# A fixed instruction order on five engines for the opening of a two-layer graph kernel

## The chip, the cores and the metric

The kernel runs on one core of one Trainium2 chip. The metric is the device time of one execution in microseconds (us). The engines are TensorE (PE; PEld is its weight load), VectorE (DVE), ScalarE (ACT), GpSimd (POOL) and SyncE (SP, which here only issues transfers). Each works through its own queue in order, and the engines wait for one another with semaphores.

## The reference

Sixty-four graphs of 256 nodes with 256 features pass through two layers; the adjacency is a 0/1 matrix. Layer 0 is a graph attention layer used twice, then a norm, a feed-forward and a second norm:

```
def _gat(h, adj, W, a, out_features):
    Wh = h @ W;  Wh1 = Wh @ a[:F];  Wh2 = Wh @ a[F:]
    e = leaky_relu(Wh1 + swapaxes(Wh2, 1, 2), 0.2)
    att = softmax(where(adj > 0, e, NEG), axis=1)
    return att @ Wh
h = _gat(_gat(x, adj, W1, a1), adj, W2, a2)
h = layernorm(x + h)
h = layernorm(h + relu(h @ w_ff1 + b_ff1) @ w_ff2 + b_ff2)
```

Layer 1 is relational attention with 8 heads (q, k, one set of values for each relation, of which only relations 0 and 1 occur with a 0/1 adjacency), an output projection, a norm, a feed-forward with gelu, and a norm. All of it is in float32.

## The kernel before

**Units and turns.** Two graphs make a unit of four tiles of 128 nodes; there are 32 units. `turn(y, x, z)` does one software-pipelined step: layer 1 of unit y, layer 0's feed-forward of unit x = y + 1, and the two graph attentions of unit z = y + 2. Inside a turn the order of PE, SP, DVE and ACT is written by hand. The 32 turns are not touched by the change.

**The opening.** Before the first turn the kernel has to load and prepare the weights, and bring unit 0 through all of layer 0, and unit 1 through its two attentions up to the sum that its first norm takes. For each unit these stages are:

- transposes of the adjacency (L726) and of x (L674) on PE, with copies by ACT and DVE;
- `project` (L741 on PE, `xpp`; copies L743 on ACT to `xp`);
- `first_scores` (rows of scores, L750 on PE), the softmax: L767 on ACT (broadcast sums), L769 on DVE (leaky relu), L772 on ACT (exp), L776 on DVE (mask and sum), L780 (reciprocal, with a small sum on POOL), L792 on ACT (scaling of `xp`);
- `first_sums` (L801 on PE, `hpp`; copies L803 on ACT to `hp`), then the same softmax on `hp`;
- `second_sums` (L812 on PE, `ygp`; L815 on DVE adds to `y`);
- the norm: L827 and L828 on DVE (moments), L838 and L839 on POOL (power -1/2), L846 on DVE (`offsets`), L856 on ACT (`applied_norm`).

Unit 0 goes on with the transposes of the normed y (L674, `h1T0`), `first_hidden` (fourteen product steps on PE, L900, each two matmuls; L912 copies on ACT, L909 sums on DVE; relu on ACT), `HiddenOut` (seven products, L989; L975 sums and L997 on DVE), a norm, and transposes `h2T0`. A row of the transposed features is set to one (`with_ones`, a memset on POOL, L686), since the biases of the projections are folded into the weights there. Turn 0 then starts with `Projections`: the steps q1, v1, q2, v2, ... (L1056 on PE), with differences `tq` on DVE (L1024). q1 and v1 read the first half of the features, q2 and the differences need the half with the row of ones.

**The weights.** The dense products use a seven-product scheme for two-by-two blocks, so each weight needs four block sums, made on POOL (`seven`, L573 to L576, and `seven_out`, L585 to L588). The norms' scale and shift are folded into the weights that follow: `shifted` (PE matmuls of one column, L596, and a DVE sum, L599), `scaled` (POOL, L603), and `joined` for q, k and v (row products L613 and L617 on PE; L618, L620, L622 on DVE). `folding()` is a generator that does this in five pieces between the stages. L562 and L656 on DVE subtract the values' weights and biases of relation 0 from those of relation 1.

**What sets the order.** The loads, the set-up of the weights and the opening are traced in program order, and a planner then orders each engine's instructions. In the opening only PE and SP are held to the order as written; on DVE, ACT and POOL the planner may pull an instruction forward or push it back by its own estimate of when it is ready. Buffers come from tagged pools: `wh` (two buffers, for `xp` and `hp`), `e` and `ea` (two each), `q` and `v` (one each), six PSUM banks under one tag.

## Time and profile before

| what | us |
|---|---|
| median of 3 runs | 2977.74 (2977.12 to 2978.61) |
| the profiled execution | 2977.29 |
| its span in the trace | 2975.6 |
| PE busy in the span | 2936.1 |
| DVE, ACT, POOL busy | 2624.7, 1822.6, 635.6 |
| first L1056 of turn 0 / of turn 1 (timeline) | 103.58 / 196.46 |
| PE busy in 60 to 70 us | 5.33 of 10 |

The span runs from the first to the last instruction of the trace; the execution's time contains some 1.7 us more. In the fenced lines L741 is a line of the kernel, `xpp<-gwe,xT` is output from inputs, `x16` a number of instructions; an fp32 matmul counts as two. A line of the windows view has, for one stretch of time, the busy time of PE, PEld, DVE, ACT and POOL, the granted TensorE clock (1.00 is full), the share of the DMA engines, and GB/s. A line of the chain has start, length, engine, output and line.

### The profile page before, as it was taken

The numbers are of one execution on the slowest core, as the hardware profiler recorded it, in microseconds if no ns is written. First come the engines' busy times: TensorE is split into PE (matmuls) and PEld (weight loads), VectorE is DVE, ScalarE is ACT, GpSimd is POOL, SyncE is SP. The second block draws the span as 40 slices with busy tenths as digits, with TensorE's granted clock in tenths as the row PEclk, the third lists the DMA queues.
The fourth block names the chain that finished last, engine by engine and source line by source line (L and its number), as shares of the span: only waits on it lengthen the run. The fifth ranks groups of instructions, "written<-read, shape, count | busy, mean of one in ns | idle before, by whom it ended". The sixth has DMA issues, their size and how long they took to land.

```text
span 2975.6 us, 58457 instructions
## 1 busy us (share of the span) xinstructions
PE 2936.1 (99%) x22192; PEld 2501.2 (84%) x22192; DVE 2624.7 (88%) x5024; ACT 1822.6 (61%) x3803; POOL 635.6 (21%) x930
## 2 busy tenths in 40 slices
PE   7999999999999999999999999999999999999997
PEld 6788888888888888888888888888888888888876
DVE  5788999988999989898989999889999898989886
ACT  4466666656656666666666666666566566666653
POOL 4122121221211221211221212212112212112211
PEclk8999999999999999999999999999999999999999
DMA  5011111111111111111111112111112111111000
GB/s 151 14 32 34 36 33 26 42 35 37 35 34 28 42 35 37 32 26 40 39 35 35 33 26 42 35 36 35 36 26 42 35 37 32 27 38 35 19 10 16
DMA packets 416883, 105.36 MB, mean 35 GB/s; under 512 B 360746, under 2 KB 416084, under 8 KB 416596
## 3 DMA queue, kind: packets, MB, share of 16 engines
q1 hardware_dynamic: 415196, 100.23, 15.5%
q8 instruction: 177, 2.90, 0.4%
q0 software_dynamic: 1056, 1.05, 0.1%
q14 instruction: 110, 0.90, 0.1%
q10 hardware_dynamic: 344, 0.28, 0.0%
HBM read 56.78 MB, written 16.78 MB: 25 GB/s over the span
## 4 chain that ended last, share of the span: by engine, by line
PE 96%; DVE 2%; ACT 1%; DMA 1%; issue 0%; POOL 0%; SPq 0%; POOLq 0%; DVEq 0%; ACTq 0%
PE yf L989 26%; PE h1a L900 15%; PE h1b L900 11%; PE po L1104 8%; PE v L1056 7%; PE qk L1056 6%; PE sp L1076 5%; PE yop L812 4%; PE xpp L741 4%; PE hpp L801 4%; PE ygp L812 3%; PE zo L1107 2%; PE rows L750 1%; DMA wf<-in_L_gnn_w_ff_dram 0%; DVE s L776 0%
## 5 line engine op out<-in xcount | busy, mean ns | idle before, releaser
L1089 DVE TENSOR_TENSOR ea<-e,aT 128x1024 f32<-128x1024 f32 x256 | 307.0, 1211 | 4.2 <-ACT e L1085 4.2
L1085 ACT ACTIVATE e<-sp 128x512 f32<-128x512 f32 x512 | 277.2, 606 | 51.7 <-PE sp L1076 35.8
L856 ACT ACTIVATE y<-y,nm,rs 128x256 f32<-128x256 f32 x450 | 243.1, 596 | 98.9 <-DVE nm L846 94.2
L912 ACT COPY h<-h1b 128x512 f32<-128x512 f32 x262 | 152.7, 583 | 192.7 <-PE h1b L900 191.0
L711 POOL COPY hT<-yt 32x256 f32<-32x256 f32 x244 | 237.4, 973 | 139.0 <-DVE yt L694 131.4
L1043 ACT COPY qk<-qk 128x512 f32<-128x512 f32 x128 | 74.3, 581 | 290.4 <-PE qk L1056 289.0
L918 ACT ACTIVATE h<-h,cols 128x256 f32<-128x256 f32 x512 | 220.8, 498 | 31.4 <-DVE h L909 31.4
L909 DVE TENSOR_TENSOR h<-h1a,h 128x512 f32<-128x512 f32 x262 | 176.2, 682 | 53.1 <-PE h1a L900 43.7
L838 POOL TENSOR_SCALAR rs<-mv 128x4 f32<-128x4 f32 (+1 forms) x134 | 33.9, 253 | 872.4 <-DVE mv L828 296.7
L997 DVE TENSOR_TENSOR y<-yf,y 128x256 f32<-128x256 f32 x448 | 185.5, 414 | 34.0 <-PE yf L989 33.7
L827 DVE BATCH_NORM_STATS2 st<-y 128x6 f32<-128x256 f32 x512 | 208.3, 409 | 5.6
L1117 POOL TENSOR_TENSOR low<-low,rq 128x16 f32<-128x16 f32 x64 | 13.9, 217 | 781.8 <-DVE rq L1116 781.8
L743 ACT COPY xp<-xpp 128x260 f32<-128x260 f32 x128 | 44.2, 368 | 212.0 <-PE xpp L741 211.9
L868 DVE TENSOR_TENSOR y<-y,rb 128x1024 f32<-128x1024 f32 (+1 forms) x130 | 166.0, 1277 | 2.2
L865 DVE TENSOR_TENSOR y<-y,rg 128x1024 f32<-128x1024 f32 (+1 forms) x130 | 162.0, 1246 | 1.2 <-ACT y L856 1.1
L1094 DVE TENSOR_TENSOR es<-e 128x1024 f32<-128x1024 f32 x128 | 155.7, 1217 | 0.0
L1076 PE MATMUL sp<-qk 32*128 32x256 f32 x2048 | 146.6, 400 | 0.0
L1104 PE MATMUL po<-e,v 128*32 128x256 f32 x2048 | 136.3, 384 | 2.1 <-DVE qk L1124 2.1
L839 POOL TENSOR_TENSOR rs<-rs,mhalf 128x4 f32<-128x4 f32 (+1 forms) x134 | 134.6, 1004 | 8.4
L1104 PE MATMUL po<-ea,v 128*32 128x256 f32 x2048 | 134.0, 379 | 0.0
L1076 PEld LDWEIGHTS sp<-qk 32*128 32x128 f32 x2048 | 92.5, 184 | 47.6 <-ACT e L1085 12.8
L900 PE MATMUL h1a<-tt,wf 128*128 128x256 f32 x512 | 131.3, 380 | 0.8 <-DVE h L909 0.8
(284 smaller groups left out, 7783.9 us busy)
## 6 DMA issues: line engine op xcount, KB each, us to landing
hT<-yt SPq DMA_DIRECT2D x852, 32.0 KB, 1.9
y<-in_x_dram SPq DMA_DIRECT2D x32, 512.0 KB, 4.6
xq<-in_x_dram SPq DMA_DIRECT2D x240, 64.0 KB, 2.2
aq<-in_adj_dram SPq DMA_DIRECT2D x240, 64.0 KB, 2.4
out_dram<-y SPq DMA_DIRECT2D x30, 512.0 KB, 2.8
wf<-in_L_gnn_w_ff_dram SPq DMA_DIRECT2D x2, 1024.0 KB, 7.4
w<-in_L_gnn_W_dram SPq DMA_DIRECT2D x2, 1024.0 KB, 7.8
first<-in_adj_dram POOLq DMA_DIRECT2D x2, 512.0 KB, 8.1
```

What stands on the lines that cost most here:

```text
L711: nc.gpsimd.tensor_copy(to, at)
L812: nc.tensor.matmul(ps[:, i * F:(i + 1) * F], lhs(t, k), rhs(b, k), start=(k == 0), stop=(k == n - 1))
L827: nc.vector.bn_stats(st[:, t, :], y[:, t, :])
L856: mark["normed"] = nc.scalar.activation(y[:, t, :], y[:, t, :], AF.Identity, bias=nm[:, t:t + 1], scale=rs[:, t:t + 1])
L900: nc.tensor.matmul(ps[:, i * N:(i + 1) * N], w_[:, f * P:(f + 1) * P], m, start=first and i == 0, stop=True, skip_group_check=True)
L918: nc.scalar.activation(y, y if ps is None else ps[:, i * N:(i + 1) * N], func, bias=bi[:, f:f + 1])
L989: nc.tensor.matmul(s.ps[n][:, i * F2:(i + 1) * F2], a[:, k, i * P:(i + 1) * P], w_[:, k, :], start=n in (1, 2, 5) and i == 0 and k == 0, s ...
L1056: nc.tensor.matmul(ps[:, i * N:(i + 1) * N], l, r, start=n in (1, 2, 5) and i == 0, stop=True, skip_group_check=True)
L1076: nc.tensor.matmul(ps[a][:, j * N:(j + 1) * N], k_[hp, m, j0:j0 + P], q[hp, m, b * N:(b + 1) * N], start=True, stop=True)
L1085: nc.scalar.activation(e[:, a, :], ps[a], AF.Exp, scale=isd)
L1089: nc.vector.tensor_tensor(ea[:, a:a + 2, :], e[:, a:a + 2, :], ab[:, None, :].to_broadcast([P, 2, NB * N]), ALU.mult)
L1104: nc.tensor.matmul(po[hp, m * N:(m + 1) * N], vs[:, hp], w[:, a, j * N:(j + 1) * N], start=(n == 0), stop=(n == len(terms) - 1))
```

## The change

The opening is written out as one order for five engines (PE, SP, DVE, ACT, POOL), and the generator `folding()` goes away: its pieces stand as calls between the stages. In the new order

- unit 0's x is transposed inside the set-up of the attention weights, and its adjacency is transposed one graph at a time around `project(0)`;
- unit 0 goes through `project`, softmax, `first_sums`, softmax before `project(1)` starts; unit 1's first softmax stands among the steps of unit 0's norm, its `first_sums` between the hidden steps, its second softmax between the hidden steps and the output products;
- the POOL sums of a weight become an iterator, of which `made(ops, n)` issues the next n; they stand between the steps, and so do `shifted`, `scaled` and `joined`, whose row products on PE are issued apart from the DVE part;
- the subtractions L562 and L656 and the sums of the bias rows (L651) move from the set-up to after the first hidden steps;
- the squares that check the adjacency (L733) go to the front of ACT's order and write to a buffer of tag `ea` instead of in place; unit 1's second scores take the buffer of tag `q`;
- the transposes ahead of both feed-forward and projections are issued in halves (`turned`), followed by the copies (`features`);
- at the end, unit 1's `second_sums` is issued one graph at a time around the halves of `h2T0`, and `with_ones` is written after both POOL steps of unit 1's norm.

The arithmetic is the same; no instruction's shape changes. The diff, cut where functions only move or split:

```diff
+    def turned(src, name, blocks=range(T), ps=None):
+        if ps is None:
+            ps = [bank(f"{name}p{k}") for k in range(KB)]
+        for k in range(KB):
+            for t in blocks:
+                nc.tensor.transpose(ps[k][:, t * P:(t + 1) * P], src[:, t, k * P:(k + 1) * P], ident)
+        return ps
+    def features(name, ps, copies):
+        dst = work.tile([P, KB, TN], F32, tag="hT", name=name)
+        for k in range(KB):
+            copies[k](dst[:, k, :], ps[k])
+        return [dst[:, k] for k in range(KB)]
...
+        load_first()
...
         w1t, w2t = transposed(w1s, "gw1"), transposed(w2e, "gw2")
+        g[0]["xT"] = to_features(g[0]["y"], "xT0")
...
+    g = {u: {} for u in range(NG)}
     gwe = gat_weights()
-    g = {u: {} for u in range(NG)}
-    load_first()
...
-    nc.vector.tensor_tensor(wv[:, :, 1, :], wv[:, :, 1, :], wv[:, :, 0, :], ALU.subtract)
...
-        nc.gpsimd.tensor_tensor(s1, a21, a22, ALU.add)
-        nc.gpsimd.tensor_tensor(s2, s1, a11, ALU.subtract)
-        nc.gpsimd.tensor_tensor(s4, a12, s2, ALU.subtract)
-        nc.gpsimd.tensor_tensor(a21, a11, a21, ALU.subtract)
-        return a11, a12, a22, s1, s2, a21, s4
+        return (a11, a12, a22, s1, s2, a21, s4), iter([
+            (s1, a21, a22, ALU.add), (s2, s1, a11, ALU.subtract),
+            (s4, a12, s2, ALU.subtract), (a21, a11, a21, ALU.subtract)])
...
+    def made(ops, n=4):
+        for _ in range(n):
+            o, x_, y_, op = next(ops)
+            nc.gpsimd.tensor_tensor(o, x_, y_, op)
 
...
+    def only_row(name):
+        only = work.tile([P, 1], F32, tag="ve", name=f"{name}o")
+        nc.vector.tensor_mul(only, ident[:, one], lg2[:, KB - 1:KB])
+        return only
+    def row_products(w, name, only):
...
+        return ps, pr
+    def joined(w, bias, ps, pr):
         nc.vector.tensor_tensor(bias, bias, ps[one].rearrange("p (o f) -> p o f", o=2), ALU.add)
...
-    def folding():
-        shifted(wf1, range(FB // 2), lb1, bf1, "bf1")
-        yield
-        shifted(wf1, range(FB // 2, FB), lb1, bf1, "bf1")
-        scaled(wf1, lg1)
-        wf1s.extend(seven(wf1, "wf1"))
-        wf2s.extend(seven_out(wf2, "wf2"))
-        yield
-        joined(wqk, "wqk", brow[:, 0:2])
-        wqks.extend(seven(wqk, "wqk"))
-        yield
-        joined(wvf, "wv", brow[:, 2:4])
-        wvs.extend(seven(wvf, "wv"))
-        shifted(w1, range(FB // 2), lb3, b1, "b1")
-        yield
-        shifted(w1, range(FB // 2, FB), lb3, b1, "b1")
-        scaled(w1, lg3)
-        w1s.extend(seven(w1, "w1"))
-        w2s.extend(seven_out(w2, "w2"))
-        yield
-    fold = folding()
+    wf1s, wf1m = seven(wf1, "wf1")
+    wf2s, wf2m = seven_out(wf2, "wf2")
+    wqks, wqkm = seven(wqk, "wqk")
+    wvs, wvm = seven(wvf, "wv")
+    w1s, w1m = seven(w1, "w1")
+    w2s, w2m = seven_out(w2, "w2")
...
-    for n, (rb, v) in enumerate(((rb1, g_bf2), (rb2, t_bo), (rb3, t_b2))):
-        nc.gpsimd.tensor_add(rb, rb, row(v, None, rows[:, n, :F]))
+    shifts = [(rb, row(v, None, rows[:, n, :F]))
+              for n, (rb, v) in enumerate(((rb1, g_bf2), (rb2, t_bo), (rb3, t_b2)))]
...
-    nc.vector.tensor_tensor(brow[:, 3], brow[:, 3], brow[:, 2], ALU.subtract)
...
-    def early_first(z):
+    def early_adjacency_of(z, b):
 
         d = g[z]
-        d["aT"] = work.tile([P, T, N], I32, tag="aT", name=f"aT{z}")
-        for b in range(G):
-            ps = bank(f"aTp{z}_{b}")
-            for j in range(NB):
-                for i in range(NB):
-                    nc.tensor.transpose(ps[:, j * N + i * P:j * N + (i + 1) * P],
-                                        d["aq"][:, b * NB + i, j * P:(j + 1) * P], ident)
+        if b == 0:
+            d["aT"] = work.tile([P, T, N], I32, tag="aT", name=f"aT{z}")
+        ps = bank(f"aTp{z}_{b}")
+        for j in range(NB):
+            for i in range(NB):
+                nc.tensor.transpose(ps[:, j * N + i * P:j * N + (i + 1) * P],
+                                    d["aq"][:, b * NB + i, j * P:(j + 1) * P], ident)
+        def cast():
             nc.scalar.copy(d["aT"][:, b * NB:(b + 1) * NB, :].rearrange("p t n -> p (t n)"), ps)
-        d["xT"] = to_features(d["y"], f"xT{z}")
-    def checked(u, aq):
+        return cast
+    def checked(u, aq, to=None):
         a = aq.rearrange("p t n -> p (t n)")
-        nc.scalar.activation(a, a, AF.Square, bias=mhalf[:, 0:1], accum_out=other[:, u:u + 1])
+        nc.scalar.activation(a if to is None else to, a, AF.Square, bias=mhalf[:, 0:1], accum_out=other[:, u:u + 1])
...
-            s.s = (work.tile([P, T, N], F32, tag="v", name=f"s{u}_{l}", bufs=1) if u > 1 else
+            s.s = (work.tile([P, T, N], F32, tag="v" if u > 1 else "q", name=f"s{u}_{l}", bufs=1)
+                   if u > 1 or u + l == 2 else
...
-    with tc.manual_schedule(engines={mybir.EngineType.PE, mybir.EngineType.SP}):
-        for stage in (early_first, project, first_softmax):
-            stage(0)
-        early_first(1)
-        next(fold)
-        for stage in (project, first_softmax):
-            stage(1)
+    with tc.manual_schedule(engines={getattr(mybir.EngineType, n) for n in
+                                     ("PE", "SP", "DVE", "Activation", "Pool")}):
+        a, b = g[0], g[1]
+        def spread(m):
+            m.scores(0)
+            m.scores(1)
+        def powers(m):
+            m.exp(0)
+            m.exp(1)
+        squares = work.tile([P, HPB, NB * N], F32, tag="ea", name="squares")
+        for u in range(2):
+            checked(u, g[u]["aq"], squares[:, u * 2:u * 2 + 2].rearrange("p a n -> p (a n)"))
+        turn_a = early_adjacency_of(0, 0)
+        turn_a()
+        project(0)
+        turn_a = early_adjacency_of(0, 1)
+        turn_a()
+        first_scores(0)
+        spread(a["m"])
+        powers(a["m"])
+        b["xT"] = to_features(b["y"], "xT1", (nc.scalar.copy,) * 2)
+        for k in range(G):
+            a["m"].masks(k)
+        a["m"].shares()
+        a["m"].scaled(WH)
+        shifted(wf1, range(FB // 2), lb1, bf1, "bf1")
+        shifted(wf1, range(FB // 2, FB), lb1, bf1, "bf1")
+        onlys = [only_row(n) for n in ("wqk", "wv")]
+        scaled(wf1, lg1)
+        made(wf1m, 2)
         first_sums(0)
-        next(fold)
-        second_softmax(0)
-        first_sums(1)
-        next(fold)
-        second_softmax(1)
-        for b in range(G):
-            second_sums(0, (b,))
-            normed(0, 0, g[0]["y"], range(b * NB, (b + 1) * NB))
-        next(fold)
-        g[0]["hT"] = to_features(g[0]["y"], "h1T0")
-        for u in range(2):
-            checked(u, g[u]["aq"])
-        affine(g[0]["y"], rg1, rb1)
+        turn_b = [early_adjacency_of(1, 0)]
+        second_scores(0)
+        turn_b.append(early_adjacency_of(1, 1))
+        spread(a["m"])
+        powers(a["m"])
+        project(1)
+        for k in range(G):
+            a["m"].masks(k)
+        a["m"].shares()
+        made(wf1m, 2)
+        made(wf2m, 1)
+        first_scores(1)
+        a["m"].scaled(F)
+        for t in turn_b:
+            t()
+        second_sums(0, (0,))
+        n0 = norm(0, 0, a["y"], range(NB))
+        b["m"].scores(0)
+        second_sums(0, (1,))
+        mv = moments(0, 0, a["y"], range(NB, NB + 1))
+        offsets(*n0)
+        n1 = norm(0, 0, a["y"], range(NB, T), mv=mv, rest=range(NB + 1, T))
+        applied_norm(a["y"], *n0, range(NB))
+        b["m"].scores(1)
+        b["m"].exp(0)
+        offsets(*n1)
+        applied_norm(a["y"], *n1, range(NB, T))
+        b["m"].exp(1)
+        pqk = row_products(wqk, "wqk", onlys[0])
+        b["m"].masks(0)
+        ph = turned(a["y"], "h1T0", range(NB))
+        turned(a["y"], "h1T0", range(NB, T), ph)
+        a["hT"] = features("h1T0", ph, (nc.scalar.copy, nc.vector.tensor_copy))
         load_x(2)
         load_rows(2)
         load_adjacency(2)
-        first_hidden(0)("2a 1a 2b 1b 5a 5b 3a 3b 6a ra 6b rb 7a sa 7b sb 4a 4b")
-        first = HiddenOut(0, 0, g[0]["y"], g[0]["h1"], wf2s, out_sums(0, 0))
-        first.sums(1, 2, 4, 3)
-        first(1, 2, 5, 6, 3)
-        normed(0, 1, g[0]["y"], range(NB))
-        first(7, 4)
-        normed(0, 1, g[0]["y"], range(NB, T))
-        g[1]["n"] = norm(1, 0, g[1]["y"], mv=second_sums(1))
-        g[0]["hT"] = with_ones(to_features(g[0]["y"], "h2T0", (nc.scalar.copy,) * 2))
-        late.append((g[0]["y"], rg2, rb2))
-        next(fold)
+        steps = first_hidden(0)
+        b["m"].masks(1)
+        b["m"].shares()
+        for rb, v in shifts:
+            nc.gpsimd.tensor_add(rb, rb, v)
+        made(wf2m, 3)
+        steps("2a 1a")
+        b["m"].scaled(WH)
+        steps("2b 1b")
+        joined(wqk, brow[:, 0:2], *pqk)
+        nc.vector.tensor_tensor(brow[:, 3], brow[:, 3], brow[:, 2], ALU.subtract)
+        nc.vector.tensor_tensor(wv[:, :, 1, :], wv[:, :, 1, :], wv[:, :, 0, :], ALU.subtract)
+        made(wqkm, 4)
+        steps("5a 5b")
+        made(w2m, 2)
+        steps("3a 3b")
+        affine(a["y"], rg1, rb1)
+        pv = row_products(wvf, "wv", onlys[1])
+        joined(wvf, brow[:, 2:4], *pv)
+        first_sums(1)
+        made(wvm, 4)
+        made(w2m, 2)
+        steps("6a ra 6b rb")
+        second_scores(1)
+        steps("7a sa 7b sb 4a 4b")
+        first = HiddenOut(0, 0, a["y"], a["h1"], wf2s, out_sums(0, 0))
+        first.sums(1, 2)
+        spread(b["m"])
+        powers(b["m"])
+        shifted(w1, range(FB // 2), lb3, b1, "b1")
+        shifted(w1, range(FB // 2, FB), lb3, b1, "b1")
+        first(1)
+        first.sums(4)
+        for k in range(G):
+            b["m"].masks(k)
+        b["m"].shares()
+        b["m"].scaled(F)
+        scaled(w1, lg3)
+        made(w1m, 4)
+        first(2)
+        first.sums(3)
+        first(5, 6, 3)
+        n0 = norm(0, 1, a["y"], range(NB))
+        first(7)
+        offsets(*n0)
+        applied_norm(a["y"], *n0, range(NB))
+        first(4)
+        n1 = norm(0, 1, a["y"], range(NB, T))
+        second_sums(1, (0,))
+        ph = turned(a["y"], "h2T0", range(NB))
+        offsets(*n1)
+        applied_norm(a["y"], *n1, range(NB, T))
+        second_sums(1, (1,))
+        turned(a["y"], "h2T0", range(NB, T), ph)
+        mv = moments(1, 0, b["y"], range(NB))
+        b["n"] = norm(1, 0, b["y"], mv=mv)
+        a["hT"] = with_ones(features("h2T0", ph, (nc.scalar.copy,) * 2))
+        late.append((a["y"], rg2, rb2))
+    with tc.manual_schedule(engines={mybir.EngineType.PE, mybir.EngineType.SP}):
         for u in range(NG):
             turn(u, u + 1, u + 2)
 
```

## The prediction

> **What bounds the kernel now.** I read the page first (busy time, slices), then the start of each turn in the timeline, then the opening's chain and its 2 us windows, and last the opening's timeline queue by queue.
>
> ```profile
> span 2975.6 us, 58457 instructions
> PE 2936.1 (99%) x22192; PEld 2501.2 (84%) x22192; DVE 2624.7 (88%) x5024; ACT 1822.6 (61%) x3803; POOL 635.6 (21%) x930
> PE   7999999999999999999999999999999999999997
> ```
>
> PE is full in all but the first slice, the second at most, and the last. The rows of scores of successive units start at 151.55, 241.82 and 332.09 us in the timeline: a turn takes 90.27 us and PE has no wait in it. The change touches only what comes before the first turn, so it can win or lose only there. That opening is the first 103.6 us (chain below: the first projection of turn 0).
>
> ```profile
> 17.95 4.71 DMA wv<-in_L_gnn_Wv_dram
> 26.33 6.65 PE xpp L741 x16
> 36.95 1.93 DVE s L776 x8
> 46.02 2.55 DVE s L776 x8
> 67.13 2.04 PE h1b L900 x4
> 103.72 1.69 PE qk L1056 x4
> ```
>
> The chain of the opening jumps between DMA, DVE softmax and PE: a latency chain, not a full engine. Its PE work at full clock, by the rows, is 74.2 us from 6.2 us on (set-up 7.5, transposes 8.3 with the rows of scores, projections 7.0, first sums 7.0, second sums 6.9, one-column sums of L596 4x1.84, row products 2x2.7, hidden steps 14x0.86, their outputs 7x1.78). 103.6 - 6.2 - 74.2 = 23 us is idle time or slow clock. That is the most to be had, with 2.6 us of turn 0 (196.46 - 103.58 - 90.27).
>
> ```profile
> 22.00:24.00 2.00, 2.00 (x22) 2.00 (x19) 1.24 (x3) 1.55 (x4) 0.00 (x0) 1.00 1.03 386
> 24.00:26.00 2.00, 0.90 (x9) 0.81 (x8) 2.00 (x8) 1.92 (x4) 0.00 (x0) 0.83 1.02 362
> 26.00:28.00 2.00, 1.67 (x4) 1.38 (x5) 0.84 (x6) 2.00 (x5) 0.00 (x0) 0.50 1.06 365
> 62.00:64.00 2.00, 0.33 (x1) 0.14 (x1) 1.46 (x6) 0.22 (x1) 0.93 (x2) 0.72 0.00 0
> 102.00:104.00 2.00, 2.00 (x19) 1.93 (x18) 1.29 (x7) 0.71 (x2) 0.40 (x1) 0.96 0.00 0
> 104.00:106.00 2.00, 2.00 (x6) 1.62 (x5) 1.28 (x3) 0.55 (x1) 1.78 (x4) 0.50 0.02 4
> ```
>
> [...]The clock falls to 0.50 at 25.4 to 32.2, 42.4 to 45.9, 62.9 to 73.2 and 103.9 to 107.3 us (half-microsecond windows): multiples of 3.4 us, and about 10 us of work lost with the one in turn 0.
>
> **The change, part by part.** I work out when PE can start the third projection product (q2) of turn 0; from there on the instructions are those of before. Before, that is 106.91.
>
> *Set-up.* Eight transposes of x go ahead of the small weight products, while PE is slow: 4 of the weights' took 1.06, so +2.1, of which 1.6 shows because the end of L539 then falls behind 15.1, where matmuls quicken. L539 ends at 15.6 (before 14.0). Then the columns' transpose and 4 adjacency transposes, 0.8, in place of 2.9: project starts at 16.4 (16.91). The loads move with load_first: on SP and POOL their order stays (x second on SP; adjacency first on POOL). On ACT the copy of x is now written ahead of eight column loads. If it held them (issued from 10.1 on, over up to 5.6, landing 4.9 later as the first vector did), PE would stand up to 4.5 for the columns; if not, 0. I take 0: in this set-up, which stays with the planner, what is ready was pulled forward (DVE L616 at 14.69, POOL wf2 sums at 16.28).
>
> *First unit's chain.* xpp 3.78, 4 transposes and 4 score rows 1.1: 21.3. Scores on ACT 1.57, leaky and exp to 24.3, two x copies of unit 1 1.2, two scalings 0.85: first_sums(0) starts at 26.4, where before it started at 33.59 behind project(1). The wv subtraction, which waited 5.5 us on DVE for its load, and the two squares (1.17 each, ACT is free at 10 to 13) no longer stand in this chain. PE meanwhile does the x transposes and 32 one-column L596 instructions (2x1.84), to 26.05. first_sums is 3.5, +2.55 for slow clock (below): 32.5. Its copies no longer wait for scaled xp of unit 1 (before, rows of hp came at 41.14): 33.6. Softmax as before, POOL idle beside it (0.69 for L769, not 1.75): exps done at 36.6, unit 1's four copies 1.5, two scalings 0.85: second_sums at 39.0 (before 51.52), to 42.5.
>
> *Norm.* DVE: sum, moments; POOL 1.0; but unit 1's leaky stands ahead of the second sum and of the second offsets, and exp ahead of the copy. Each is 0.7 or less: y is normed at 48.7, its copies at 50.0. First hidden step at 50.0, before 67.13: 17.1 ahead.
>
> *Feed-forward.* Here it is given back. PE work from the first hidden step to the last second_sums of unit 1: 12.1 hidden, 12.5 outputs, 3.46 and 0.5 transposes, which were here; and moved in: row product 2.7, first_sums(1) 3.5, rows 0.55, both L596 pieces of w1 3.7 = 39.0. Waits: the row product waits on DVE for the joining of wqk (2.5), the brow and wv differences, 1.1 after the steps run dry. These two run beside POOL's wqk sums; DVE L776 beside such sums was 0.93 to 0.95 three times in four against 0.42, so +0.5 each, 1.0 in all (bounds 0 and 2.1, from the worst row below). Norm at the end 0.45. Slow clock 2.55 and 1.7. Sum: 50.0 + 39.0 + 2.55 + 4.25 = 95.8.
>
> ```profile
> 44.35 1.75 DVE L769 SCALAR_TENSOR_TENSOR s<-s 128x512 f32<-128x512 f32 x1
> 45.52 1.71 POOL L575 TENSOR_TENSOR wf1s<-wf,wf1s 128x512 f32<-128x512 f32 x1
> 105.16 0.52 POOL L686 MEMSET h2T<- 1x512 f32 x1
> 105.76 1.27 POOL L839 TENSOR_TENSOR rs<-rs,mhalf 128x4 f32<-128x4 f32 x1
> ```
>
> *A new wait.* Before, POOL set the row of ones between the two steps of unit 1's norm. Now it is written behind both. q2 and the differences on DVE need that row: sum 0.7, moments 2.15, POOL 0.25 + 1.0 + 0.52, q2 at 100.5; q1 and v1 (1.73) fit inside. Without it q2 would come 1.5 earlier. POOL's w1 sums (2.2 + 5.1) follow the shares of unit 1, about 83 to 91, ahead of the two norms' POOL steps; they delay DVE's offsets and the fourth output's sum by some 1 us, covered by PE's second_sums. Without that cover it is 1 us more. The bias rows' additions and the other sums on POOL end before they are read. No cost, with their cover: unit 1's second scores in the q buffer (turn 0's first copy into it comes after the last second_sums anyway), the squares' own buffer, the 17 loads for unit 2 on SP (landed by 47, read after 120; nothing else waits on SP).
>
> 106.91 - 100.5 = 6.4, and 0.5 in turn 0 (slow until 107.3; 0.3 before the tq product): 6.9. The profiled execution took 2977.29 (span 2975.6 and 1.7 around it): 2970.4. The median shown is 0.45 above it: 2970.8.
>
> *The clock, weighed.* In 22 to 24 PE is busy 2.00 of 2.00 and still loses the clock at 25.4; there it does transposes and L596, whose moving side is one column. At 102 to 103.9 the same again. And windows with 2.4 to 2.6 of 3.4 us of slow dense work (25.4 to 28.8, 66.3 to 69.7) did not bring it back. [...]By the trace the stretch of transposes and L596 at 20 to 26 loses it for 3.4 to 6.8 us (5.1 taken, half of it lost), the norm at 45 to 50 again, and w1's 3.7 us of L596 between hidden steps and outputs costs one window, 1.7. I follow the trace; the phase of the windows is not mine to know.
>
> **The rivals.** (a) As summed: 2970.8, own range 2967.5 to 2974; chance 0.50. (b) The clock holds in two or three of the spells, and the wait for the ones is hidden: 2962 to 2967, taken 2964.0; for it, one L596 piece next to dense work kept full clock at 37 to 39; against it, the pieces now come in pairs. 0.22. (c) The gain is spent on queues: column loads 4.5 late, 1.1 more beside POOL, POOL's 1 us uncovered: 6.6 of 6.9 gone, 2977.4 (2974 to 2979). For it, fixed orders on DVE and POOL let one late release hold all behind it; against, the first unit's chain is short and mostly free of POOL. 0.24. (d) Slower: PE stays slow through the feed-forward. In place 49 to 97 us there are 14 windows; each slow one costs 1.7, two and a half are counted. A window that is only about three quarters busy does not reopen the clock, and the added steps make PE wait for DVE. Four more slow windows use up the gain, eight more make it 0.2% slower; 2984. Against it, before went back to full at 73.2 after one full window of the same steps. 0.04.
>
> **How the numbers follow.** 0.2% is 6.0 us, about what a measurement here can tell from no change: faster means below 2971.8. Of (a) two thirds lie there, with all of (b) and a little of (c): 0.62. Same 0.34, slower 0.04. The range drops the far end of (b), (d) and most of (c).
>
> **What would show it.** Right: first_sums(0) at about 26, with no project(1) ahead of it; h1b's first matmul near 50; clock 0.50 near 26 and again after w1's L596; the ones' MEMSET just ahead of q2, q2 near 100; next turns 90.27 apart. Wrong: the columns' transpose after 17; h1b beyond 56; no slow spell at all; POOL's w1 sums ending beyond 93; any wait of PE in the later turns.

## The result, and the profile after

The changed kernel takes 2970.66 us (median of 8 runs, 2966.56 to 2973.35). The kernel before, on the same chips, takes 2977.43 (2975.66 to 2980.26): 6.8 us less, a ratio of 0.9976 with a 95% interval of 0.9965 to 0.9987. The forecast was 2970.8. Line numbers have moved: L741 is now L750, L801 is L811, L812 is L822, L900 is L910, L989 is L999, L1056 is L1066, L596 is L623, L603 is L630, L769 and L776 are L779 and L786, L792 is L802, L839 is L849, the POOL sums (L573 to L588) are L616, and L562 is L1644. In an experiment they differ from these by a few lines where its edit adds or takes some away.

The page of the profiled execution (2973.35 us, the slowest of the eight), its span, busy times and PE's slices:

```profile
span 2971.6 us, 58462 instructions
PE 2935.6 (99%) x22192; PEld 2502.4 (84%) x22192; DVE 2620.0 (88%) x5023; ACT 1823.7 (61%) x3804; POOL 637.3 (21%) x930
PE   8999999999999999999999999999999999999997
```

The busy times are those of before within 5 us. Only PE's first slice is fuller, 8 where it was 7: the change acts there alone. From the chain of the opening:

```profile
24.98 5.43 PE hpp L811 x16
47.54 2.04 PE h1b L910 x4
57.47 1.11 DVE wv L1644
82.35 3.16 POOL w L630 x2
101.54 1.13 PE qk L1066 x4
```

The first sums of unit 0 start at 24.98 (before 33.59), the first hidden step at 47.54 (67.13), q2 of turn 0 at 101.54 (106.91). Of 19.6 us that the first hidden step is ahead, q2 keeps 5.4. Some 9 of the 14.2 given back are PE work that only changed places: by the rows, the values' row product (2.8), the first sums of unit 1 (3.6), rows of scores (0.6) and half of w1's one-column products (2.3) now stand behind the first hidden step. The chain's links in between show where it leaves PE on the way: at the values' subtraction on DVE and at POOL's scaling for w1. One point of the list of the change needs a correction: `project(1)` starts at 31.57, beside unit 0's second softmax (its broadcast sums start at 31.33) and not behind it. What the gain rests on is that it stands behind unit 0's first sums; before, it stood in front of them (26.33 in the prediction's chain), and they came at

```profile
33.59 3.65 PE L801 MATMUL hpp<-xp,s 128*128 128x258 f32 x16
```

The rows of scores of the next turns start at 146.06 and 236.33, so a turn still takes 90.27.

The clock, in the 2 us windows of the changed kernel:

```profile
24.00:26.00 2.00, 1.68 (x9) 1.40 (x10) 0.69 (x7) 1.90 (x5) 1.34 (x3) 0.82 0.96 334
26.00:28.00 2.00, 2.00 (x6) 1.52 (x6) 0.00 (x0) 0.51 (x2) 1.92 (x2) 0.50 1.07 379
72.00:74.00 2.00, 2.00 (x16) 2.00 (x16) 1.97 (x4) 1.74 (x6) 0.00 (x0) 0.76 0.00 0
74.00:76.00 2.00, 2.00 (x10) 2.00 (x11) 0.75 (x3) 1.18 (x2) 0.00 (x0) 0.50 0.00 0
104.00:106.00 2.00, 2.00 (x22) 1.26 (x21) 1.19 (x4) 1.31 (x3) 0.00 (x0) 1.00 0.04 8
```

At half clock are 25.3 to 28.7, 45.7 to 52.6 and 73.0 to 79.9: five windows of 3.4 us, where before had seven (two at 25.3, one at 42.4, three at 62.9, one at 103.8). The one at 104 is gone. In the 3.4 us up to 73.05 PE is busy 3.40, and the clock then falls to 0.50; the 32 one-column products of w1 run from 70.59 to 75.16. The rows that answer to the steps booked beside POOL's sums and to the new wait, from the timeline of DVE and POOL:

```profile
32.20 1.42 DVE L779 SCALAR_TENSOR_TENSOR s<-s 128x512 f32<-128x512 f32 x2 [7.21 <-ACT s L777]
97.15 0.43 DVE L1034 TENSOR_TENSOR tq<-h2T 128x256 f32<-128x256 f32 x1 [0.56 <-ACT h2T L523]
99.89 1.02 POOL L849 TENSOR_TENSOR rs<-rs,mhalf 128x4 f32<-128x4 f32 x1
100.97 0.52 POOL L692 MEMSET h2T<- 1x512 f32 x1
```

Two leaky steps together take 1.42, where before one took 1.75 beside POOL's sum (the prediction's row at 44.35). And the row of ones is set at 100.97, just ahead of q2. The longest of PE's waits in the first 104 us, but for the 6.2 for the first load, which before has too (total, times, longest):

```profile
PE qk L1066 <- POOL h2T L692: 2.4, 1, 2.4
PE h1T0p L516 <- ACT y L866: 2.2, 4, 1.6
PE wvbp L644 <- DVE wv L1644: 1.3, 1, 1.3
```

The first and the third are waits that the new order made; for the normed y PE waited 4.4 before.

### The profile page after: what moved, and what is told of

Same layout as the page of the kernel before. It is cut to its first block, busy times and chain, and to the rows that moved or that the text cites. A ratio compares the mean times of both kernels' runs of the same rounds, so it can differ in the third digit from the quotient of the medians.

```text
span 2971.6 us, 58462 instructions
## 1 busy us (share of the span) xinstructions
PE 2935.6 (99%) x22192; PEld 2502.4 (84%) x22192; DVE 2620.0 (88%) x5023; ACT 1823.7 (61%) x3804; POOL 637.3 (21%) x930
## 4 chain that ended last, share of the span: by engine, by line
PE 96%; DVE 2%; ACT 1%; POOL 1%; issue 0%; DMA 0%; ACTq 0%; POOLq 0%; DVEq 0%
PE yf L999 26%; PE h1a L910 15%; PE h1b L910 11%; PE po L1114 8%; PE v L1066 7%; PE qk L1066 6%; PE sp L1086 5%; PE hpp L811 4%; PE yop L822 4%; PE xpp L750 4%; PE ygp L822 4%; PE zo L1117 2%; PE rows L759 1%; DVE st L837 0%; ACT y L866 0%
## 5 line engine op out<-in xcount | busy, mean ns | idle before, releaser
L1095 ACT ACTIVATE e<-sp 128x512 f32<-128x512 f32 x512 | 277.2, 605 | 52.6 <-PE sp L1086 37.0
L849 POOL TENSOR_TENSOR rs<-rs,mhalf 128x4 f32<-128x4 f32 (+1 forms) x134 | 134.4, 1003 | 8.3
L910 PE MATMUL h1a<-tt,wf 128*128 128x256 f32 x512 | 131.2, 380 | 0.8 <-DVE h L919 0.8
```

What stands on the lines that cost most here:

```text
L910: nc.tensor.matmul(ps[:, i * N:(i + 1) * N], w_[:, f * P:(f + 1) * P], m, start=first and i == 0, stop=True, skip_group_check=True)
L1095: nc.scalar.activation(e[:, a, :], ps[a], AF.Exp, scale=isd)
```

## How the runs are compared

Every kernel was timed against the kernel before on the same chip; the medians of before are 2976.83 to 2977.46 in these groups. A single profile compares less well, because the set-up runs at two speeds. From the timeline of the changed kernel, and of an experiment with the same instructions there on PE (e9 below):

```profile
11.38 3.79 PE L567 MATMUL gwep<-gw2e,gw1t 128*128 128x260 f32 x8
```
```profile
10.82 2.02 PE L567 MATMUL gwep<-gw2e,gw1t 128*128 128x260 f32 x8
```

The same eight matmuls take 3.79 or 2.02, and the first projection then starts at 15.8 or 13.4. So the table gives, beside the medians, the time from the first projection of unit 0 to the rows of scores of unit 2 in turn 0 ("opening", one profile each), which leaves the set-up out. Among the variants of the changed kernel the intervals of most neighbours overlap (e2 and e3 with the change itself, too); there the opening is the better guide, and the medians mix set-ups of both speeds.

| kernel | median, us (runs) | ratio to before (95%) | first_sums(0) after project(0) | opening |
|---|---|---|---|---|
| before | 2977.43 (8) | 1 | 16.68 | 134.64 |
| after | 2970.66 (8) | 0.9976 (0.9965 to 0.9987) | 9.21 | 130.29 |
| e4: PE, SP held | 2977.38 (13) | 0.9999 (0.9991 to 1.0007) | 17.42 | 136.86 |
| e9: PE, SP, POOL held | 2977.53 (13) | 1.0000 (0.9992 to 1.0008) | 14.44 | 137.38 |
| e7: all but POOL held | 2978.71 (13) | 1.0006 (0.9998 to 1.0015) | 9.22 | 136.70 |
| e10: all but ACT held | 2972.10 (21) | 0.9982 (0.9975 to 0.9988) | 9.52 | 130.20 |
| e6: subtractions in set-up | 2972.80 (21) | 0.9987 (0.9981 to 0.9994) | 11.19 | 131.19 |
| e2: 64 columns | 2966.03 (5) | 0.9965 (0.9951 to 0.9979) | 9.22 | 127.00 |
| e5: before, 64 columns | 2981.30 (21) | 1.0014 (1.0007 to 1.0020) | 16.94 | 137.56 |
| e1: row of ones first | 2971.30 (9) | 0.9978 (0.9968 to 0.9988) | 9.21 | 130.93 |
| e3: values early | 2968.19 (7) | 0.9970 (0.9958 to 0.9981) | 9.21 | 126.52 |
| c3: e2 and e3 | 2967.69 (6) | 0.9967 (0.9954 to 0.9979) | 9.22 | 124.84 |
| c2: c3, end with w1 last | 2967.30 (6) | 0.9968 (0.9956 to 0.9980) | 9.21 | 125.32 |
| c4: c3, end with POOL re-ordered | 2961.85 (5) | 0.9948 (0.9934 to 0.9962) | 9.22 | 121.10 |

## Experiments: whose order carries the gain

The change holds five engines to one order. Theory: the gain comes from what no longer stands in front of unit 0's chain on DVE, and from POOL's sums no longer running beside the softmax. Rival: it comes from PE's new order, which any planner would have served. The first run gives DVE, ACT and POOL back to the planner, with the new program otherwise whole:

```diff
-    with tc.manual_schedule(engines={... ("PE", "SP", "DVE", "Activation", "Pool")}):
+    with tc.manual_schedule(engines={... ("PE", "SP")}):
```

> The changed kernel's program, but only PE and SP are held to the written order; DVE, ACT and POOL are left to the planner, as before. If the gain comes from PE's order (unit 0's chain first), most of it stays: 4 to 7 us under the kernel before. If it comes from holding DVE, ACT and POOL, most goes: within 2 us of before, or above it. By the built order POOL's sums of wf2 and w2 come early again and lie beside DVE's softmax steps, and the values' subtraction stands ahead of the first leaky relu again: I expect q2 1 to 3 us later than in the changed kernel, unless the row of ones is set earlier.

It took 2977.38: the whole gain is gone. Groups of instructions on DVE in the first 60 us of e4 (line, operation, tiles, count | busy, mean ns | idle before them):

```profile
L786 DVE SCALAR_TENSOR_TENSOR s<-s,aT 128x256 f32<-128x256 f32 x12 | 8.6, 748 | 0.3 <-ACT s L782 0.2
L779 DVE SCALAR_TENSOR_TENSOR s<-s 128x512 f32<-128x512 f32 x6 | 4.9, 811 | 6.2 <-ACT s L777 6.2
```

In the changed kernel the means are 422 and 687 ns. The planner ran POOL's scaling and sums for wf beside the masks of unit 0's first softmax (three of the four took 1.47 each), and put the values' subtraction in front of its first leaky relu, where DVE waited for the load until 24.31; the broadcast sums had begun at 20.53 and take 1.57. In the kernel before the same subtraction waited in the same place:

```profile
22.76 0.69 DVE L562 TENSOR_TENSOR wv<-wv 128x512 f32<-128x512 f32 x1 [5.46 <-DMA wv<-in_L_gnn_Wv_dram]
```

DVE stood 5.46 us for the load, and the leaky relus, next in its queue, started at 23.37.

In e4 first sums started 17.42 after the projection, no better than before.

The next run takes POOL alone out of the list, the one after it leaves POOL in and takes DVE and ACT out.

```diff
+    with tc.manual_schedule(engines={... ("PE", "SP", "DVE", "Activation")}):    # e7
+    with tc.manual_schedule(engines={... ("PE", "SP", "Pool")}):                 # e9
```

> The changed kernel, with POOL left to the planner and PE, SP, DVE and ACT held. By the built order POOL does wf2's four sums at 17 to 22 us and w2's four beside the softmaxes of unit 0, where the changed kernel has POOL empty. If the meeting of DVE's two-input steps with POOL's sums is what the fixed order avoids (1.47 against 0.42 us for each mask step in the run where only PE and SP were held), unit 0's chain to the first hidden step is 3 to 6 us later and the time goes up by 2 to 5 us; the row of ones is set before the norm's power there, worth up to 1 us. If not, the same time within 1 us.

> The new program with PE, SP and POOL held to the order as written in the opening, and DVE and ACT left to the planner. If the place of POOL's sums carries the gain, DVE's softmax steps run as in the changed kernel (L786 at 0.42 to 0.45 each, L779 at about 0.7), the first sums of unit 0 come 2 to 3 us later than 24.98, since the planner puts the values' subtraction ahead of the first leaky relu and DVE waits for its load, and the net gain stays: 2971 to 2974. If the orders of DVE and ACT carry it, the gain goes again: 2976 or more. If all three are needed together, something between, about 2975.

Neither keeps anything: 2978.71 and 2977.53. In e7 the first sums are as early as in the changed kernel (9.22), and the loss comes at the second softmax. DVE's and POOL's timeline of e7:

```profile
33.76 1.76 DVE L779 SCALAR_TENSOR_TENSOR s<-s 128x512 f32<-128x512 f32 x1
35.44 1.49 DVE L786 SCALAR_TENSOR_TENSOR s<-s,aT 128x256 f32<-128x256 f32 x1
```
```profile
33.36 1.60 POOL L616 TENSOR_TENSOR w2t<-w,w2t 128x512 f32<-128x512 f32 x1
34.93 1.71 POOL L616 TENSOR_TENSOR w<-w 128x512 f32<-128x512 f32 x1
```

Sums of w2, wanted only in turn 0, were pulled forward onto the softmax of unit 0: the leaky step takes 1.76 instead of 0.71, a mask 1.49 instead of 0.42, and POOL's own sum 1.71 instead of 1.27. Second sums come 25.1 after the projection, where the changed kernel has 20.3, and the clock is lost for six windows between 38.8 and 86.6 instead of four. That is more than was expected: the first hidden step is 6.4 later (3 to 6) and the median 8.0 above the changed kernel (2 to 5).

In e9 DVE's steps take what they take in the changed kernel (L786 416 ns for 422; of six L779 one meets a POOL sum and takes 1.28), as its first theory said, and still the gain is gone. The timeline of DVE and of PE in e9:

```profile
23.61 0.69 DVE L1644 TENSOR_TENSOR wv<-wv 128x512 f32<-128x512 f32 x1 [9.87 <-DMA wv<-in_L_gnn_Wv_dram]
```
```profile
27.88 6.60 PE L811 MATMUL hpp<-xp,s 128*128 128x258 f32 x16 [5.55 <-ACT xp L802]
```

DVE stood 9.9 us for a load that nothing in unit 0's chain needs. PE waited 5.6 us for the shares behind it, lost the clock (three windows from 23.4), and took 6.60 for sums that take 3.75 at full clock (e2): 14.44 from project to first sums instead of 9.21. Its first theory had the start right (27 to 28 was expected) and the net wrong (2971 to 2974): the start was reached from a set-up that ended 2.3 us earlier, so the delay is 5.2 and not 2 to 3. The load is not the whole loss: later PE waits 4.0 for a DVE sum ahead of an output product, where the changed kernel waits 0.5.

That leaves DVE and POOL together, with ACT free:

```diff
+    with tc.manual_schedule(engines={... ("PE", "SP", "DVE", "Pool")}):          # e10
```

> The new program with PE, SP, DVE and POOL held in the opening and ACT alone left to the planner, which moves the copies of unit 1 and its first broadcast sums to other places. If the orders of DVE and POOL together are what is needed, first_sums(0) starts within 0.5 us of 24.98, the first hidden step within 1.5 of 47.54, and the net stays at 2970 to 2973. If ACT's order is the missing part of the run with POOL held, ACT's exps and copies come late between DVE's softmax steps, the first hidden step starts beyond 50, and the net is 2975 or more.

2972.10, opening 130.20: the first theory. The first sums start at 23.05 and the first hidden step at 45.19, out of the stated bounds around 24.98 and 47.54 only by the fast set-up (9.52 and 31.66 after the projection, for 9.21 and 31.77). Where the planner put ACT's copies of unit 1 did not matter. So the gain needs DVE's order and POOL's order at once; each without the other brings nothing (e7, e9), since the chain is held by whichever of the two is left out.

One more run asks how much the moved subtractions alone are worth in the fixed order: L1643 and L1644 back in the set-up, where DVE's order now holds them.

```diff
+    nc.vector.tensor_tensor(wv[:, :, 1, :], wv[:, :, 1, :], wv[:, :, 0, :], ALU.subtract)   # set-up
...
-        nc.vector.tensor_tensor(brow[:, 3], brow[:, 3], brow[:, 2], ALU.subtract)
-        nc.vector.tensor_tensor(wv[:, :, 1, :], wv[:, :, 1, :], wv[:, :, 0, :], ALU.subtract)
```

> The changed kernel, with one part undone: the subtractions of relation 0 from relation 1 (weights L562 and bias L656 of before) stand in the set-up again, so on DVE the first waits for its load (about 22.7 us) ahead of unit 0's first leaky relu, which was ready at 21.3. If that in-order wait is part of the gain: first_sums(0) starts 2 to 3 us later (27 to 28 instead of 25.0), PE's wait of 1.3 us at 57 us goes, net 0.5 to 2 us slower than the changed kernel. If PE's other work covers it: no change or 1 us faster.

2972.80, 2.1 us above the changed kernel, with intervals that overlap. First sums come 2.0 later after the projection and the clock falls for two windows at 26.1 instead of one, but the wait of the values' row product at 57 is gone and gives part of it back: the opening is 0.9 longer. Held to a fixed order, the subtraction in front of the chain costs far less than what e9 lost (7.1 in the opening).

## Experiments: the clock

Theory, an estimate from the rows at 70 to 76 of the changed kernel (PE busy 3.40 in the 3.4 us up to 73.05, one-column products from 70.59 on, then clock 0.50): the spell goes with the one column that each of these matmuls streams. Rival: spells follow PE's waits, the pieces cost nothing, and nothing changes within 0.5 us. The moving side is widened from one to 64 equal columns, of which one is used; the figures put on record are the theory's:

```diff
-                nc.tensor.matmul(ps[:, f:f + 1], w[:, k, f * P:(f + 1) * P], shift[:, k:k + 1],
+                nc.tensor.matmul(ps[:, n:n + 64], w[:, k, f * P:(f + 1) * P],
+                                 shift[:, k:k + 1].to_broadcast([P, 64]),
```

> The changed kernel, with the moving side of the L596 matmuls (L623 in the changed kernel) widened from 1 to 64 equal columns; their count, their weight loads and the results are the same. [...]the slow spell after w1's piece (73 to 80 us) goes away, and the one at 25 to 29 too: about 3.4 + 1.7 us of slow clock saved less a few tenths for longer matmuls, 3 to 5 us under the changed kernel. [...]If the pieces themselves get longer by over 1 us, the widening isn't free and the test is void.

2966.03, 4.6 us less than the changed kernel (3.3 in the opening), for more work on PE. A window and a row of PE's timeline of e2:

```profile
72.00:74.00 2.00, 2.00 (x20) 2.00 (x20) 2.00 (x5) 0.00 (x0) 0.00 (x0) 1.00 0.04 8
```
```profile
66.34 3.68 PE L624 MATMUL b1sp<-cols,w 128*128 128x64 f32 x32
```

The 32 products take 3.68 with 64 columns, and take 3.63 with one (the piece for wf in e9, at full clock); PEld is busy 2.00 of the 2.00 us from 68 to 70, in the middle of them. That the weight load and not the width sets their pace is an estimate from these figures. The spells at 25 and at 73 are gone, the one in the norm stays (PE busy 1.56 in the 3.4 us before it), and a single window at 95.8 appears behind the wait for the ones. The rival is out: PE's waits are those of the changed kernel (2.4 for the ones, 1.3 for the values, 2.0 for the normed y), and the spells are not.

Nor is it the place of the windows or the speed of the set-up. In all eight profiles of the new program with one column a slow spell begins 2.4 to 4.7 us after w1's piece starts; in none of the three with 64 columns and the piece in the same place (e2, c3, c4) does one come within 10 us. And c2 (below) has the slow set-up and wide products for wf at 21.19, the changed kernel the narrow ones at 21.03; only the changed kernel loses the clock at 25.3. Widths between 1 and 64 were not run.

The same edit in the kernel before:

> The kernel before, with only the moving side of its L596 matmuls widened from 1 to 64 equal columns. If what streams through the array decides the clock, two of its slow spells go, at 25 to 32 and at 104 to 107 us (10.2 us of slow clock, of which some 8 were PE work): 3 to 4 us faster than before. The two spells behind real gaps (42 and 63 us) stay. If the changed kernel gained 4.6 us from the same edit for another reason (its own order), the kernel before stays within 1 us.

It missed: 2981.30, 4.5 us slower, with an opening 2.9 longer. Of the two windows at 25.3 the second stays (29.1 to 32.5); the one at 103.8 is gone, but one comes at 111.0, and another at 2886.1 near the end. Two things moved with the edit. The values' load was there only at 24.30 (22.76 in the profile before), so that the softmax behind it is 1.5 later and PE waits 2.8 us for unit 1's copy of x instead of 1.4; the order on DVE and ACT is the same there, and from one profile each it is not known whether the edit has a part in this. And the planner, which still orders POOL, set the row of ones earlier (103.62) and both scalings of w1 ahead of the power of unit 1's norm, which now starts at 107.46 (105.76): DVE's offsets wait for it, its sums for q stand behind them, and PE waits 2.3 for these and then loses a window. So here an edit to an instruction's shape did not stay alone, and this run neither supports nor refutes the theory.

## Experiments: the waits that the new order made

First the row of ones, written ahead of the two POOL steps of unit 1's norm:

```diff
+        a["hT"] = with_ones(features("h2T0", ph, (nc.scalar.copy,) * 2))
         mv = moments(1, 0, b["y"], range(NB))
         b["n"] = norm(1, 0, b["y"], mv=mv)
-        a["hT"] = with_ones(features("h2T0", ph, (nc.scalar.copy,) * 2))
```

> One part undone: the row of ones is set on POOL before unit 1's norm instead of behind it; nothing else differs from the changed kernel. If the wait for that row holds PE (2.4 us before q2 of turn 0 in the changed kernel's trace), q2 comes 2 to 2.5 us earlier, at about 99.2 us, and the time is 2 to 2.5 us under the changed kernel's (about 2968). If the wait is cover for something else (DVE's moments and tq behind it), q2 moves by less than 0.5 us and the next step waits instead: the same time within 0.5 us.

2971.30: nothing. The wait of 2.4 at q2 is gone, and q2 comes 2.6 earlier after the projection, but the list of PE's waits at 90 to 112 us has a new one at q's third product:

```profile
PE qk L1066 <- DVE qk L1050: 1.7, 1, 1.7
```

DVE stands in the offsets of unit 1, behind the power that POOL now does later, and the sums for q are queued behind them. That takes 1.6 of the 2.6 back. The rest goes to the clock, which falls at 101.2 to 104.7 in this run and not in the changed kernel: a product of v takes 2.04 there for 1.06. Both theories hold in part: q2 moves as in the first, and the next step waits as in the second.

Then the values: their subtraction right after the first softmax, their row product in the norm's gap, and the joining of q and k ahead of unit 1's masks (a move of four lines).

> The changed kernel, with the values' subtraction on DVE straight after unit 0's first softmax, the row product of the values' weights in the gap of PE behind that of wqk (about 42 us), and the joining of wqk ahead of unit 1's masks. If PE's wait on DVE for the subtraction (1.3 us at 57 us) and the empty stretch in unit 0's norm (42 to 47.5) are what is left on the path, 2.8 us of PE work and 1.3 of wait leave the feed-forward, and the clock stays at 1.00 at 46 to 52.7 (3.4 us): 4 to 7 us under the changed kernel. If the end of the opening is set by DVE and POOL (w1's sums, norms) and not by PE, under 2 us.

2968.19, 2.5 less than the changed kernel (3.8 in the opening), between its two theories; the wait of 1.3 is gone, and three windows of slow clock are left of five (at 25.3, 56.0 and 73.1). PE now waits 2.0 for a copy of a hidden step on ACT, so not all of it stays.

The two together:

> The changed kernel with two of the earlier edits together: the one-column products of L596 streamed with 64 equal columns, and the values' subtraction, their row product and the joining of q and k earlier. If what both take away lies on the same path, the gains add (4.6 and 2.5 us): 2962 to 2964, and the next turn starts near 138. If the end of the opening is set by POOL's sums for w1 and the row of ones, both edits only make PE wait there longer: about 2966, a wait on the row of ones beyond 3 us, and the next turn at 140 or later.

The two do not add. Against the changed kernel the opening is 5.45 us shorter, for 3.29 and 3.77 apart, and the median, 2967.69, is no better than that of e2 alone: the six runs fall at 2965.9 (two) and 2967.3 to 2968.3 (four). Neither theory fits: the wait for the ones stays at 2.4, and does not grow beyond 3 as the second had it. The profiled run, one of the two at 2965.9, is 0.1 us ahead of e2's with an opening 2.2 shorter; 0.5 of that is a later start, and the rest is lost at the very end, ahead of turn 31. Windows of 3.4 us, of e2 and of c4 (below), at the same point of the program:

```profile
2869.40:2872.80 3.40, 1.48 (x6) 1.16 (x7) 1.73 (x4) 3.31 (x5) 1.10 (x2) 1.00 0.43 154
2872.80:2876.20 3.40, 3.40 (x21) 3.04 (x21) 3.12 (x6) 3.39 (x10) 0.52 (x1) 1.00 0.00 0
```
```profile
2863.40:2866.80 3.40, 1.49 (x6) 1.16 (x7) 1.73 (x4) 3.32 (x5) 1.10 (x2) 0.98 0.43 154
2866.80:2870.20 3.40, 3.40 (x13) 2.94 (x13) 2.21 (x4) 3.39 (x10) 0.00 (x0) 0.51 0.00 0
```

The same gap, 1.5 of 3.4 us busy, costs the next window in one run and not in the other (21 matmuls against 13). c3 has that slow window at 2870.9 too; the changed kernel is spared there and pays at a later gap, with a slow window at 2916.4. What differs is where the gap falls between the points at which slow spells start. In the changed kernel's trace they start at 25.26, 45.74, 73.05 and 2916.35 us, which are 6, 8 and 833 times 3.413 us apart, and last 3.413 or 6.827; the two in c4, at 50.7 and 2866.7 by its 2 us windows, are 825 times 3.413 apart. Counted on from its own spell at 95.8, such a point falls at 2870.8 in e2 (an estimate), inside PE's gap (2869.4 to 2871.3); in c4 the gap (2863.4 to 2865.3) lies whole within the 3.413 us that end at 2866.7, where its spell starts. That this place decides is my estimate from these two runs; no run moved the gap alone. The price of the spell, by c3 against e2, is some 1.6 us (2.2 - 0.5 - 0.1). The four higher times of c3 are not explained by it: their granted clock (0.998 to 0.999) is no lower than that of the other two (0.998). The slow set-up, which that reading leaves out, costs some 2.4 us (the first projection at 15.8 for 13.4) and would fit, but they have no trace.

Last, the end of the opening. c2 keeps the edits of c3, moves unit 1's second sums and first moments ahead of unit 0's last output product and w1's one-column products behind it, and puts w1's scaling and sums at the very end:

> A combination: L596 widened to 64 columns; the values' subtraction and row product early, as in the run of that name; and the end of the opening reordered: unit 1's second_sums and its norm go ahead of unit 0's last output product, and w1's L596 pieces move behind it, where PE waits for unit 0's last norm; w1's scaling and sums come last on POOL. By the sum: 2.4 us of PE's wait for the row of ones and 3.5 us of slow clock leave, 2.5 us from the values: 7 to 10 us under the changed kernel, 2961 to 2964. If the end is bound by DVE or by POOL's sums running into turn 0, 4 to 6 us, as from the widening and the values alone.

2967.30, no better than c3 and short of both theories (3.4 us under the changed kernel, for 7 to 10 or 4 to 6). The wait for the ones is gone, but DVE's sum and moments of unit 1 now stand ahead of the sum that frees a bank for the last output product (PE's waits at 60 to 112 us of c2):

```profile
PE yf L1002 <- DVE y L1010: 4.1, 2, 2.4
```

c4 leaves PE's order as in c3 and moves only what POOL and DVE do: the ones before the norm, w1's scaling and sums last, unit 1's first moments before unit 0's last offsets.

```diff
-        scaled(w1, lg3)
-        made(w1m, 4)
...
         second_sums(1, (0,))
         ph = turned(a["y"], "h2T0", range(NB))
+        mv = moments(1, 0, b["y"], range(NB))
         offsets(*n1)
...
-        mv = moments(1, 0, b["y"], range(NB))
-        b["n"] = norm(1, 0, b["y"], mv=mv)
         a["hT"] = with_ones(features("h2T0", ph, (nc.scalar.copy,) * 2))
+        b["n"] = norm(1, 0, b["y"], mv=mv)
         late.append((a["y"], rg2, rb2))
+        scaled(w1, lg3)
+        made(w1m, 4)
```

> The same two edits, and the end in another order: the row of ones is set ahead of the norm of unit 1, the scaling and the sums for w1 come last on POOL, and the moments of unit 1's first half stand ahead of the last offsets of unit 0. If the waits at the end are only a matter of POOL's order, they leave PE and 1.5 to 3 us more are gained: 2960 to 2963. If POOL's sums for w1, now beside turn 0, slow DVE's differences, or the wait passes to the next reader on DVE as it did when the row of ones alone was moved, it is no faster than without the third edit: 2963 to 2967, with a wait of PE on DVE of 1 to 3 us in the first steps of turn 0.

2961.85 (2961.23 to 2962.23), the fastest: a ratio of 0.9948 (0.9934 to 0.9962), 15 us below before and 9 below the change as given (9.2 in the opening). The wait for the ones is gone, and what PE waits for DVE in the first steps of turn 0 is 0.4. The step that failed in e1 works here because POOL is free when the moments come: its last power for unit 0 ends 71.5 us after the first projection (in the changed kernel 79.0), with w1's 8.4 us of work behind it instead of in front.

## Why the prediction was right

**The likeliest case came in**, at 2970.66 against 2970.8, inside its own range of 2967.5 to 2974. Rival (c), in which queues eat the gain, is out for the change as made; but its kind of loss is what happened in e4, e7 and e9, and near its number (2977.4). Rival (d) is out: five slow windows, fewer than before. Rival (b) did not happen by itself, but e2 brought about the half of it that concerns the clock: without two of the spells the time was 2966.0, where (b) had 2962 to 2967, with the wait for the ones still there. The clock as it was weighed held: slow windows came at all three places named (25.3, 45.7 and 73.0). The 2964.0 taken for (b) was an estimate of mine.

**Steps that held.** The end of L539 was given as 15.6 (measured 15.2), project as 16.4 (15.8), first_sums(0) as 26.4 (25.0). The columns' transpose came at 15.11, so ACT's copy did not hold the column loads. The wait of the row product on the subtraction was put at 1.1 (1.31), with 1.0 for steps beside POOL's sums: wv's subtraction took 1.10 beside them (0.69 in before, with POOL busy 0.00 in that window of 2 us). Turns are 90.27 apart. The sum puts q1 near 97.3 (97.17).

**Steps that missed, and cancelled.**

- Second_sums at 39.0 and h1b at 50.0 came at 36.11 and 47.54. Of the 2.9 at second_sums, 0.6 is the set-up and 0.6 the clock in first_sums (5.43 for 3.5 + 2.55). The other 1.6 is ACT: its copies of unit 1 were booked on the path with 2.7 in all, and for the most part they ran beside DVE's masks. The norm then took 0.4 more than I had.
- From the first hidden step to the last second_sums I had 45.8; it took 48.0 (95.5 - 47.54). On PE's row, 1.7 of the 2.2 is the clock after w1's one-column products: one window was counted (1.7), two came. The work itself was 0.9 more than the 39.0 booked, and PE's waits were 0.4 less (2.15 for 2.55): the 1.0 booked for steps beside POOL's sums did not show as a wait of its own. POOL's work for w1 ran from 82.35 to 90.8, as booked.
- From there to q2 I had 4.7; it took 6.0. The sum and moments were 2.85 in my working, and DVE needed 4.0 from 95.56: the first tq of turn 0 stands among the moments (the row at 97.15) and DVE waits 0.56 for its input and spends 0.43. So the wait at q2 was 2.4, not 1.5.

Two and a half early, 2.2 and 1.3 late: q2 was 1.0 late, a gain of 5.4 there for 6.4. The half microsecond granted to turn 0 was 0.1 in the trace: 5.5 in all, for 6.9.

**What the number hid.** Of the 5.5 us by which the profiled execution is ahead after the opening, it keeps 3.9 (2977.29 to 2973.35); a slow window at 2916.4, which the profile before does not have, takes the rest. The prediction had PE without waits after the opening; the last two turns have some in both kernels (2.1 and 2.0 us the longest), and there such windows are lost or not. The median of eight gained 6.8. What the forecast took from one trace leaves open the number of such windows in a run: the runs of the changed kernel spread over 6.8 us, and those with the higher mean clock are the faster ones (0.997 in the fastest, 0.995 in the slowest); the speed of the set-up comes on top and was not in the forecast. The interval of the ratio is some 3 us wide on either side. So the mechanism was right, its size in the trace 1.4 us less than summed, and that the median hit within 0.2 us is luck.

## What to carry to other kernels

When a planner shares a latency chain with work that is off it, fix the order of every engine that can get in front of the chain: here leaving out POOL (e7), or DVE with ACT (e9), took the whole gain. After such a change, list PE's waits again and ask of each what is queued behind it; moving one step (e1) passed the wait to the next reader, moving the block of work that sat in front of it (w1's sums in c4) removed it. And where PE's row is full and the clock still falls, look at how many columns stream: in e2 the wider matmuls cost 0.05 us a piece (3.68 for 3.63), and the clock read 1.00 at 72 to 76, where the changed kernel has 0.76 and 0.50; in the kernel before the same edit gave no gain (e5, 2981.30).

## What the runs showed of the hardware that I had not expected

- Thirty-two fp32 matmuls (as the trace counts them) take 3.68 us with 64 moving columns and 3.63 with one, yet in the new program a slow spell begins within 4.7 us of the start of w1's narrow ones in all eight profiles, and within 10 us of the wide ones in none of three; e2 is 4.6 us faster than the changed kernel.
- Where a mask or a leaky step of DVE ran beside a POOL sum, both took longer: a mask 1.47 for 0.42 (e4), a leaky step 1.76 for 0.71 and POOL's sum 1.71 for 1.27 (e7). Whether POOL's order was fixed or planned decided between 2970.7 and 2978.7 (the changed kernel and e7).
- The set-up runs its eight L567 matmuls in 2.02 or 3.79 us in different executions of the same instructions, while the granted clock in those windows reads 1.00 in both. In the changed kernel the step comes at 15.1, three windows of 3.4 us before the first slow spell at 25.3; that the slow set-up ran at half clock, unseen in the row, is an estimate from this and from the ratio of the two times (1.88).
